# Layer 2 of a four-layer graph kernel: x2 turned on VectorE, h in x2's place, a seventh kept block, and another order of the last stores

## The chip, the cores and the metric

The kernel runs on one core of a Trainium2 chip. The metric is the device time of one execution in microseconds (us); lower is better. A core has TensorE (PE; its weight loads are listed as PEld), VectorE (DVE), ScalarE (ACT), GpSimd (POOL) and SyncE (SP), which here only issues transfers, on memory SBUF for operands and PSUM for matmul results. Transfers from every queue run on the core's 16 DMA engines.

## The reference

There are 3327 nodes of 64 features and one weighted adjacency `adj` of 3327 x 3327. Four layers follow each other, each ending in a residual and a layer norm. Cut to what matters:

```python
# layer 0:  x = LN(x + (1 - 0.1 * x - 0.01 * sum(x * (adj @ x))))
# layer 1:  hyperbolic attention over all pairs (i, j), weighted by
#           sigmoid(left_i + right_j) * adj
x = _layernorm(x + _L1_gnn_ref(x, adj, L1_gnn_att_W, L1_gnn_att_b))

# layer 2: two rounds over the whole adjacency
def _L2_gnn_ref(user_embs, adj, W):
    x = user_embs
    for k in range(2):
        agg = adj @ x
        x = jnp.tanh(jnp.concatenate([agg, x], axis=1) @ W[k])
    return x
x = _layernorm(x + _L2_gnn_ref(x, adj, L2_gnn_W))

# layer 3: the last 100 neighbours of each row, weights 0.5 ** (places from the end)
out = w @ (x @ weight) + bias
x = _layernorm(x + out)
```

## The kernel before

The host hands in the transposed adjacency, padded to 3328 x 3328: 26 blocks of 128 rows (the source nodes), each 128 partitions x 13312 bytes. A block is read from HBM several times: in layer 1, in both rounds of layer 2 and in layer 3. Some are kept in SBUF: `EARLY` = 4 blocks (25 to 22) from the beginning, and `LATE` = 2 blocks (20, 21) from the end of layer 1 until the end of layer 2.

Features are held in two forms: by node (128 nodes on the partitions, 26 x 64 values along a row) and stacked in columns (two halves of 64 features on the partitions, 1664 nodes along a row). `x2`, layer 1's result, is made by node in the last lines of `near_end` (L1554 to L1558) on VectorE; `lj` holds x2 times the first half of round 1's weights, made by TensorE and VectorE beside it.

**Layer 2** (`layers`, from L308) has two rounds, `k` = 0 and 1. Each adds up, in four PSUM chunks `acc[c]` of 416 nodes, one product per block and chunk (`add`, L400; two matmuls, one for each half of the nodes), so 26 blocks, and a part from the features themselves (`bottom`, L393: the second half of the weights times `hT`, x2 in columns). `tanh` (L493) writes h, the round's result, to `nxt`. `nxt` is a tile `hT` of the pool `cols` (two buffers of 128 x 1664 f32); layer 3's `accT` comes from the same pool.

In round 1 `hT` is x2 in columns and is written over the tile `xc` (`x2T`, L363): `turned(i)` (L383) transposes a group of three nodes' blocks on TensorE into PSUM, and ScalarE copies it out. Its five calls stand behind the fourth and fifth blocks, and `bottom` and a small Tanh (it loads the table) behind the sixth (L472 to L486).

Blocks that are not kept are streamed: four buffers in the pool `strm` (tag `at`, `UNDER_WAY` = 4), loaded ahead at the end of layer 1 by `blocks_ahead` (L1750), and two in the pool `more` (tag `bt`). The order of TensorE is written out by hand:

```python
order = list(ready)
for i, jb in enumerate(stay):
    order += [jb] + others[i * share : (i + 1) * share]
```

The `ready` blocks come first, then each kept block followed by `share` streamed ones; the blocks in `end` (two in round 1, three in round 2) are added chunk by chunk at the close, each chunk followed by its `tanh`. Before, round 1 is 0 to 3, 25, 4 to 7, 24, 8 to 11, 23, 12 to 15, 22, 16 to 19, and 20, 21 at the close: 16 streamed beside the four ready. Round 2 begins with the last six streamed blocks, which are still there, then 5 others, 20, 3 others, 21, 3 others, 25, 3 others, and closes with 24, 23, 22: 14 streamed. All loads stand in SP's queue in this order; a load waits until TensorE has consumed the block that lay in its buffer.

**Layer 1** (`near_sphere`, L989) runs over pairs of blocks and column chunks. Its left sides `lb` (128 x 3328 f32) are read by the sigmoid (L1052, listed as L1051) of each pair; the streamed half blocks `at` of the pool `n1r` (four buffers, on the right side of SBUF) are read by GpSimd (L1062). The order of its second half puts the kept blocks last, so no `at` is wanted in its last eight steps. The pools `late` and `strm` lie on the right, too, and take the room that layer 1's tiles leave.

**Layer 3's end** (`last_out`, L796) norms the last 1664 rows in three parts of 6, 4 and 3 node blocks and stores each; the last node block has only 127 rows and is stored alone (L828). `rsqrt_of` (L540) takes the root: one VectorE operation, ScalarE's Sqrt, a reciprocal and four VectorE operations.

Of the kernel before, what the change touches and what calls it, by code (L numbers as in the profile page):

```python
# [10 lines left out]
F32 = mybir.dt.float32  # L11
# [4 lines left out]
ALU = mybir.AluOpType  # L16
# [3 lines left out]
P = 128  # L20
# [17 lines left out]


EARLY = 4  # L40
LATE = 2
UNDER_WAY = 4

LN_EPS = 1e-5
MIN_NORM = 1e-15
# [28 lines left out]
def kernel(  # L74
# [232 lines left out]

    @with_exitstack  # L308
    def layers(ctx, x2, x3, begun_here, kept, ready, ahead_ctx, strm):
        cols = ctx.enter_context(tc.tile_pool(name="cols", bufs=2, reuse_waits="tile"))  # L310

        more_ctx = ExitStack()
        more = more_ctx.enter_context(tc.tile_pool(name="more", bufs=2, reuse_waits="tile"))
        l3m = None
        in_order = ctx.enter_context(ExitStack())
        in_order.enter_context(tc.manual_schedule(engines={mybir.EngineType.PE}))
# [20 lines left out]
            nc.vector.tensor_scalar(mask[q], at, 0.0, None, ALU.not_equal)  # L337

        groups = fours

        def to_stack(ps, src, dst, g, n, copy, name):

# [34 lines left out]
        with tc.tile_pool(name="l2p", bufs=2, space=PSUM, reuse_waits="tile") as l2p:  # L377
            for k in range(2):
                hw = lj
                nxt = cols.tile([P, HALF], F32, tag="hT", name=f"hT_{k + 1}")  # L380
                begun = set()

                def turned(i):  # L383
# [44 lines left out]
                if k == 0 and not begun_here:  # L428
                    turned(0)
                    turned(1)  # L430
                    top(0, nc.scalar.copy)
                    turned(2)
                    top(1)
                    for c in range(CPH):
                        add(c, order[0])
                    turned(3)
                    top(2)
                    turned(4)
                    top(3)
                    for c in range(CPH):  # L440
                        add(c, order[1])
                    top(4)
                    for c in range(CPH):
                        bottom(c)

                    warm_t = small.tile([P, 1], F32, tag="warm", name="warm_t")
                    nc.scalar.activation(warm_t, ones, AF.Tanh)
                    order = order[2:]
                elif k:
                    top(0)  # L450
                    bottom(0)
                    bottom(1)
                    top(1)
                    bottom(2)
                    for c in range(CPH - 1):
                        add(c, order[0])
                    top(2)
                    bottom(CPH - 1)
                    add(CPH - 1, order[0])
                    top(3)  # L460
                    order = order[1:]
                seen, held = {}, {}
                for i, jb in enumerate(order):
                    if jb not in blocks:
                        if len(seen) % (UNDER_WAY + 2) < 2 and (k == 0 or len(seen) < 2):
                            blocks[jb] = held[jb] = block(more, jb, tag="bt", name=f"bt_l2_{k}_{jb}")
                        else:
                            blocks[jb] = block(strm, jb, tag="at", name=f"at_l2_{k}_{jb}")
                        seen[jb] = blocks[jb]
                    for c in range(CPH):  # L470
                        add(c, jb)
                    if k == 0 and begun_here:  # L472

                        if i == 3:
                            turned(0)
                            turned(1)
                        if i == 4:
                            turned(2)
                            turned(3)
                            turned(4)  # L480
                        if i == 5:
                            for c in range(CPH):
                                bottom(c)

                            warm_t = small.tile([P, 1], F32, tag="warm", name="warm_t")
                            nc.scalar.activation(warm_t, ones, AF.Tanh)  # L486
                    if k and jb in held and len(held) == 2:
                        for q in range(AHEAD + 3):
                            masks(q)
                def chunk_end(c):  # L490
# [6 lines left out]
                for c in range(CPH):  # L497
                    chunk_end(c)

                last = sorted(list(seen)[-UNDER_WAY - 2 :], key=lambda jb: jb not in held)  # L500
                ready = {jb: seen[jb] for jb in last}
                hT = nxt

# [227 lines left out]

        def sums_out(h):

            accT = cols.tile([P, HALF], F32, tag="hT", name=f"accT_{h}")
            to = [
                accT[:, 2 * c * CW : 2 * (c + 1) * CW].rearrange("p (e k) -> p e k", e=2)
                for c in range(2)
            ]
            nc.scalar.activation(to[0], acc[h, 0], AF.Identity, bias=b3_sb)
            nc.vector.tensor_scalar(to[1], acc[h, 1], b3_sb, None, ALU.add)  # L740
            return accT
# [54 lines left out]
        def last_out(h, accT):  # L796

            xh, hh, sh = in_half(h)
            v = small.tile([P, NBH], F32, tag="v_out", name=f"v_out_{h}")
            parts = (slice(0, 6), slice(6, 10), slice(10, NBH))  # L800
            prs = [places(t) for t in (*banks, acc_tile(f"pr_o_{h}"))]
            for pr, s in zip(prs, parts):
                by_node(accT, pr, s)

            def added(k):
                s = parts[k]
                nc.vector.tensor_tensor(hh[:, s], prs[k][:, : s.stop - s.start], xh[:, s], ALU.add)
                nc.scalar.activation(sh[:, s], hh[:, s], AF.Square)

            def summed(k):  # L810
                s = parts[k]
                nc.vector.tensor_reduce(v[:, s], sh[:, s], axis=AX.X, op=ALU.add)

            added(0)
            added(1)
            summed(0)
            added(2)
            summed(1)
            summed(2)
            r = rsqrt_of(v, NBH)  # L820

            rows = N - h * HALF - (NBH - 1) * P
            for s, queue in zip(parts, (nc.sync, nc.scalar, nc.sync)):
                nc.vector.tensor_tensor(
                    hh[:, s], hh[:, s], spread(r[:, s], s.stop - s.start), ALU.mult
                )
                if store(queue, h, hh, s):
                    nc.scalar.dma_start(out[N - rows :], hh[:rows, NBH - 1])  # L828

        first_out = None  # L830
        with_step = [
# [42 lines left out]
    with tc.tile_pool(name="l1", bufs=1) as l1:  # L874
# [114 lines left out]
        def near_sphere(mT, ljT_0, xm, sq_e, t_e, rows_63):  # L989
# [3 lines left out]
            with tc.tile_pool(name="n1", bufs=1, reuse_waits="tile") as n1, tc.tile_pool(  # L993
# [1 line left out]
            ) as n1w, tc.tile_pool(  # L995
                name="n1c", bufs=1, space=PSUM, reuse_waits="tile"
            ) as n1c, ExitStack() as pairs:

                n1r = pairs.enter_context(
                    tc.tile_pool(name="n1r", bufs=4, side="right", reuse_waits="tile")  # L1000
                )
                first_ps = ExitStack()
                n1p = first_ps.enter_context(
                    tc.tile_pool(name="n1p", bufs=1, space=PSUM, reuse_waits="tile")
# [5 lines left out]
                ri = mT.rearrange("p (n d) -> p n d", d=D)  # L1010
                riT = n1.tile([P, HALF], F32, name="riT")

                lb = n1.tile([P, NP], F32, name="lb")
                lfT = n1.tile([NB, P], F32, name="lfT")
                lf_rows = dram.tile([NB, P], F32, name="lf_rows")

# [733 lines left out]
        def blocks_ahead(arm):  # L1750
# [6 lines left out]
                tc.tile_pool(name="strm", bufs=UNDER_WAY, side="right", reuse_waits="tile")  # L1757
            )
            all_kept, ready = dict(kept), {}
            for jb in range(NB - EARLY - LATE, NB - EARLY):  # L1760
                all_kept[jb] = block(late, jb, name=f"kept_{jb}")
            for jb in range(UNDER_WAY):
                ready[jb] = block(strm, jb, tag="at", name=f"at_l2_0_{jb}")
            return all_kept, ready, ahead_ctx, strm
# [60 lines left out]
```

## Time and profile before

| What | us |
|---|---|
| median of 3 runs | 561.71 |
| the runs | 560.8, 561.71, 563.36 |
| the profiled execution | 562.28 |
| its span, first to last instruction | 560.5 |
| TensorE busy | 527.3 (94%) |
| VectorE busy | 368.2 (66%) |
| ScalarE busy | 278.1 (50%) |
| GpSimd busy | 215.7 (38%) |
| layer 2's first block begins on TensorE | 241.93 |
| layer 2's second round, first block begins | 324.71 |
| layer 3's first product after layer 2 | 398.28 |

The mean granted TensorE clock was 0.987 of full speed. In the profile "L12" is line 12 of the kernel; a group is written as line, engine, operation, output <- inputs, shapes, and how often. An idle time is put down to the work that ended it ("<-"). Transfers moved 145.27 MB, 259 GB/s on average over the span. Times of single instructions count from the span's start.

### The profile page before, as it was taken

To read this page: it belongs to the slowest core of one execution; us is meant where nothing else is said; L and a number is where in the kernel's file an instruction comes from. 1 tells how busy PE (TensorE), PEld (TensorE's weight loads), DVE (VectorE), ACT (ScalarE), POOL (GpSimd) and SP (SyncE) were. 2 spreads that over 40 slices of the span, in tenths; PEclk is the share of its full clock that TensorE was granted. 3 is DMA by queue.
4 is the path that set the end of the run, shared out by engine and by line. 5 is a ranking of instruction groups with operands and counts; after the bars stand their busy time and mean duration, and the time that the engine had idled before them with its cause. 6 is when DMAs were issued, how large, how long until landed. Compare 5 with 4: busy or idle time off the path is not lost.

```text
span 560.5 us, 7513 instructions
## 1 busy us (share of the span) xinstructions
PE 527.3 (94%) x2854; PEld 226.6 (40%) x2854; DVE 368.2 (66%) x532; ACT 278.1 (50%) x328; POOL 215.7 (38%) x138
## 2 busy tenths in 40 slices
PE   8989989999999999999999999998989999999992
PEld 5522222222222222854444444443455555545542
DVE  6899999999999999791000011300478878787834
ACT  4899999999999998612000100000274333343311
POOL 3799999999999999200000000000011000000000
PEclk9899999999999999899999999999999999999997
DMA  8976766676766715699999149996609996789701
GB/s 305 353 273 205 234 209 204 222 233 199 238 205 223 235 32 222 272 425 425 425 426 424 43 148 417 425 425 291 244 8 343 342 303 227 237 258 358 274 2 36
DMA packets 34037, 145.27 MB, mean 259 GB/s; under 512 B 10285, under 2 KB 11975, under 8 KB 28871
## 3 DMA queue, kind: packets, MB, share of 16 engines
q1 hardware_dynamic: 31655, 144.11, 69.8%
q10 hardware_dynamic: 2336, 0.59, 0.5%
q8 instruction: 24, 0.39, 0.3%
q14 instruction: 22, 0.18, 0.1%
HBM read 143.23 MB, written 0.87 MB: 257 GB/s over the span
## 4 chain that ended last, share of the span: by engine, by line
PE 61%; DVE 20%; ACT 8%; DMA 6%; issue 3%; DVEq 0%
PE cnt L403 20%; PE pq L1075 12%; DVE v L1096 12%; PE cnt L513 11%; PE acc L709 6%; DMA at_l<-in_adjT 5%; ACT sg L1051 4%; PE acc L724 3%; ACT pq L1088 3%; DVE a L1087 2%; DVE w L526 1%; PE cnt L394 1%; DVE mask L337 1%; DMA x<-in_x 1%; PE pm L1367 1%
## 5 line engine op out<-in xcount | busy, mean ns | idle before, releaser
L1062 POOL TENSOR_TENSOR u<-sg,at 128x832 f32<-128x832 f32 x88 | 170.0, 1964 | 3.5 <-ACT sg L1051 3.0
L1075 PE MATMUL pq<-riT,ljT 64*128 64x416 f32 x416 | 100.2, 560 | 15.2 <-DVE v L1096 6.2
L1087 DVE SCALAR_TENSOR_TENSOR a<-pq,dl,u 128x832 f32<-128x832 f32 x104 | 111.9, 1077 | 2.9 <-PE pq L1075 2.8
L1088 ACT ACTIVATE pq<-pq,al,gas 128x832 f32<-128x832 f32 x104 | 105.0, 1011 | 15.1 <-DVE a L1087 14.2
L1096 DVE SCALAR_TENSOR_TENSOR v<-pq,a 128x832 f32<-128x832 f32 x104 | 105.7, 1016 | 1.1 <-ACT pq L1088 0.8
L1108 PE MATMUL acc<-v,xv 128*64 128x416 f32 x416 | 95.4, 537 | 0.1
L403 PE MATMUL cnt<-at_l,lj 128*64 128x416 f32 x480 | 86.1, 513 | 2.3 <-DMA at_l<-in_adjT 2.3
L1051 ACT ACTIVATE sg<-lb,rb 128x1664 f32<-128x1664 f32 (+1 forms) x53 | 87.3, 1647 | 0.1
L528 ACT ACTIVATE w<-cnt 128x832 int16<-128x832 f32 x55 | 47.3, 863 | 71.5 <-PE cnt L513 71.4
L640 POOL TENSOR_TENSOR s<-sq,s 128x384 bf16<-128x384 f32 (+1 forms) x4 | 4.1, 1028 | 200.3 <-ACT s L639 200.3
L493 ACT ACTIVATE hT<-cnt 128x416 f32<-128x416 f32 x8 | 4.1, 517 | 138.3 <-PE cnt L403 138.3
L1075 PEld LDWEIGHTS pq<-riT,ljT 64*128 64x128 f32 x416 | 31.5, 184 | 88.3 <-DVE v L1096 83.1
L526 DVE TENSOR_SCALAR w<-cnt 128x832 int16<-128x832 f32 x49 | 50.1, 1023 | 25.8 <-PE cnt L513 24.5
L403 PEld LDWEIGHTS cnt<-at_l,lj 128*64 128x64 f32 x480 | 34.1, 137 | 52.1 <-issue 47.3
L513 PE MATMUL cnt<-mask,tri 128*128 128x416 bf16 x208 | 53.5, 339 | 0.1
L709 PE MATMUL acc<-w,s 128*128 128x416 bf16 x208 | 52.6, 339 | 0.5 <-DVE hid L781 0.5
L513 PE MATMUL cnt<-mask,rest 128*128 128x416 bf16 x200 | 51.6, 340 | 1.2 <-ACT w L528 0.6
L391 DVE COPY lj<-pn_l 128x512 f32<-128x512 f32 (+1 forms) x4 | 2.4, 592 | 73.9 <-PE pn_l L355 73.9
L1108 PEld LDWEIGHTS acc<-v,xv 128*64 128x64 f32 x416 | 20.6, 134 | 61.0 <-issue 57.8
L337 DVE TENSOR_SCALAR mask<-ah 128x1664 bf16<-128x1664 f32 x42 | 43.4, 1034 | 0.0
L403 PE MATMUL cnt<-kept,lj 128*64 128x416 f32 x192 | 35.5, 514 | 0.0
L1062 POOL TENSOR_TENSOR u<-sg,kept 128x832 f32<-128x832 f32 x16 | 31.0, 1972 | 2.6 <-ACT sg L1051 2.6
(282 smaller groups left out, 403.7 us busy)
## 6 DMA issues: line engine op xcount, KB each, us to landing
at_l<-in_adjT SPq DMA_DIRECT2D x26, 1664.0 KB, 13.7
at<-in_adjT SPq DMA_DIRECT2D x44, 832.0 KB, 4.9
ah<-in_adjT SPq DMA_DIRECT2D x42, 832.0 KB, 6.3
bt_l<-in_adjT SPq DMA_DIRECT2D x8, 1664.0 KB, 12.8
kept<-in_adjT SPq DMA_DIRECT2D x6, 1664.0 KB, 8.7
lb<-lf_rows SPq DMA_DIRECT2D x2, 384.0 KB, 4.5
ljT<-ljT SPq DMA_DIRECT2D x4, 128.0 KB, 6.2
x<-in_x ACTq DMA_DIRECT2D x1, 416.0 KB, 5.5
```

The source lines that it names most:

```text
L337: nc.vector.tensor_scalar(mask[q], at, 0.0, None, ALU.not_equal)
L403: nc.tensor.matmul(acc[c][h * D : (h + 1) * D, :], hw[:, slot(jb), :], blocks[jb][:, o : o + CW], start=c not in begun, stop=last, skip_gr ...
L513: nc.tensor.matmul(cnt[c][:, e, :], mat, mask[q][:, of], start=start, stop=(mat is tri), skip_group_check=True,)
L526: nc.vector.tensor_scalar(w.bitcast(I16), cnt[c], 0.0, None, ALU.max)
L709: nc.tensor.matmul(acc[h, c][:, e, :], s12[:, slot(jb)].rearrange("p t d -> p (t d)"), ws[q, c][:, e, :], start=first, stop=last,)
L1051: nc.scalar.activation(sg[:, :, of], lbs[:, :, of], AF.Sigmoid, bias=rb[:, sl : sl + 1])
L1062: nc.gpsimd.tensor_tensor(u, sg[:, :, of], at[:, :, of], ALU.mult)
L1075: nc.tensor.matmul(pq[:, h, :], ljT[h != jb // NBH][rows, of], riT[rows, ch * CW : (ch + 1) * CW], start=True, stop=True,)
L1087: stt(a_s[t], pqs[t], dl[:, one], us.pop(t), op0=ALU.add, op1=ALU.mult)
L1088: nc.scalar.activation(pqs[t], pqs[t], AF.Square, bias=al[:, one], scale=gas[:, one])
L1096: stt(w, pqs.pop(t), CUBIC_REST, a_s.pop(t), op0=ALU.add, op1=ALU.mult)
L1108: nc.tensor.matmul(accs[cp, ci][h * D : (h + 1) * D, :], xv[:, slot(jb), :], w[:, h, :], start=(jb == orders[cp][0]), stop=(jb == orders[c ...
```

## The change

Six edits in one:

1. x2 is turned to columns by VectorE (`turned_by_squares`): sixteen instructions, each turning thirteen squares of 32 x 32 (32 partitions, 416 values). They stand at the head of round 1, behind x2's last addition on VectorE's queue. The TensorE transposes and ScalarE copies go. `bottom` moves behind the ninth block, and the small Tanh there reads a column of `hT`.
2. `cols` is no pool any more but another view of `x2`: both rounds' h and layer 3's `accT` are written there.
3. `LATE` is 3: block 19 is kept as well. Its place is that of `lb`, which moves to a pool of its own on the right beside `n1r`. The loads of 20 and 21 are issued first, then that of 19.
4. With that, `blocks_ahead` and `order` make other sequences. Round 1: 0 to 3, 25, 4 to 6, 24, 7 to 9, 23, 10 to 12, 22, 13 to 15, 20, 16 to 18, closing with 21, 19 (15 streamed). Round 2: six ready, 5 others, 20, 3 others, 21, 3 others, 19, 2 others, 25, closing with 24, 23, 22 (13 streamed).
5. In `last_out` the root is written out with one VectorE operation less, the factor -0.5 going into the last product.
6. The last three parts are multiplied and stored in the reverse order, and the 127 rows are stored first, on ScalarE's queue.

`MORE` = 2 only names a number that stood there.

```diff
--- before.py
+++ after.py
@@ -38,8 +38,9 @@
 
 
 EARLY = 4
-LATE = 2
+LATE = 3
 UNDER_WAY = 4
+MORE = 2
 
 LN_EPS = 1e-5
 MIN_NORM = 1e-15
@@ -307,10 +308,11 @@
 
     @with_exitstack
     def layers(ctx, x2, x3, begun_here, kept, ready, ahead_ctx, strm):
-        cols = ctx.enter_context(tc.tile_pool(name="cols", bufs=2, reuse_waits="tile"))
+
+        cols = x2.rearrange("p n d -> p (n d)")
 
         more_ctx = ExitStack()
-        more = more_ctx.enter_context(tc.tile_pool(name="more", bufs=2, reuse_waits="tile"))
+        more = more_ctx.enter_context(tc.tile_pool(name="more", bufs=MORE, reuse_waits="tile"))
         l3m = None
         in_order = ctx.enter_context(ExitStack())
         in_order.enter_context(tc.manual_schedule(engines={mybir.EngineType.PE}))
@@ -338,6 +340,20 @@
 
         groups = fours
 
+        def turned_by_squares(src, dst):
+
+            Q = 32
+            to = dst.rearrange("p (n k) -> p n k", k=P)
+            for h in range(2):
+                for f in range(D // Q):
+                    rows = slice(h * D + f * Q, h * D + (f + 1) * Q)
+                    for q in range(P // Q):
+                        nodes = slice(q * Q, (q + 1) * Q)
+                        nc.vector.transpose(
+                            out=to[rows, :, nodes],
+                            in_=by_half(src)[nodes, :, h, f * Q : (f + 1) * Q],
+                        )
+
         def to_stack(ps, src, dst, g, n, copy, name):
 
             pt = ps.tile([P, 4 * P], F32, tag="pt", name=f"pt_{name}_{g}")
@@ -377,7 +393,7 @@
         with tc.tile_pool(name="l2p", bufs=2, space=PSUM, reuse_waits="tile") as l2p:
             for k in range(2):
                 hw = lj
-                nxt = cols.tile([P, HALF], F32, tag="hT", name=f"hT_{k + 1}")
+                nxt = cols
                 begun = set()
 
                 def turned(i):
@@ -446,6 +462,8 @@
                     warm_t = small.tile([P, 1], F32, tag="warm", name="warm_t")
                     nc.scalar.activation(warm_t, ones, AF.Tanh)
                     order = order[2:]
+                elif k == 0:
+                    turned_by_squares(x2, hT)
                 elif k:
                     top(0)
                     bottom(0)
@@ -462,7 +480,7 @@
                 seen, held = {}, {}
                 for i, jb in enumerate(order):
                     if jb not in blocks:
-                        if len(seen) % (UNDER_WAY + 2) < 2 and (k == 0 or len(seen) < 2):
+                        if len(seen) % (UNDER_WAY + MORE) < MORE and (k == 0 or len(seen) < MORE):
                             blocks[jb] = held[jb] = block(more, jb, tag="bt", name=f"bt_l2_{k}_{jb}")
                         else:
                             blocks[jb] = block(strm, jb, tag="at", name=f"at_l2_{k}_{jb}")
@@ -471,20 +489,13 @@
                         add(c, jb)
                     if k == 0 and begun_here:
 
-                        if i == 3:
-                            turned(0)
-                            turned(1)
-                        if i == 4:
-                            turned(2)
-                            turned(3)
-                            turned(4)
-                        if i == 5:
+                        if i == 8:
                             for c in range(CPH):
                                 bottom(c)
 
                             warm_t = small.tile([P, 1], F32, tag="warm", name="warm_t")
-                            nc.scalar.activation(warm_t, ones, AF.Tanh)
-                    if k and jb in held and len(held) == 2:
+                            nc.scalar.activation(warm_t, hT[:, :1], AF.Tanh)
+                    if k and jb in held and len(held) == MORE:
                         for q in range(AHEAD + 3):
                             masks(q)
                 def chunk_end(c):
@@ -497,7 +508,7 @@
                 for c in range(CPH):
                     chunk_end(c)
 
-                last = sorted(list(seen)[-UNDER_WAY - 2 :], key=lambda jb: jb not in held)
+                last = sorted(list(seen)[-UNDER_WAY - MORE :], key=lambda jb: jb not in held)
                 ready = {jb: seen[jb] for jb in last}
                 hT = nxt
 
@@ -731,7 +742,7 @@
 
         def sums_out(h):
 
-            accT = cols.tile([P, HALF], F32, tag="hT", name=f"accT_{h}")
+            accT = cols
             to = [
                 accT[:, 2 * c * CW : 2 * (c + 1) * CW].rearrange("p (e k) -> p e k", e=2)
                 for c in range(2)
@@ -817,15 +828,25 @@
             added(2)
             summed(1)
             summed(2)
-            r = rsqrt_of(v, NBH)
+
+            r0, r = (small.tile([P, NBH], F32, tag=f"last_{k}", name=f"last_{k}") for k in range(2))
+            nc.vector.tensor_scalar(v, v, 1.0 / D, LN_EPS, ALU.mult, ALU.add)
+            nc.scalar.activation(r0, v, AF.Sqrt)
+            nc.vector.reciprocal(r0, r0)
+            nc.vector.tensor_tensor(r, v, r0, ALU.mult)
+            nc.vector.tensor_tensor(r, r, r0, ALU.mult)
+            nc.vector.scalar_tensor_tensor(r, r, -3.0, r0, op0=ALU.add, op1=ALU.mult)
 
             rows = N - h * HALF - (NBH - 1) * P
-            for s, queue in zip(parts, (nc.sync, nc.scalar, nc.sync)):
-                nc.vector.tensor_tensor(
-                    hh[:, s], hh[:, s], spread(r[:, s], s.stop - s.start), ALU.mult
+
+            for s, queue in zip(parts[::-1], (nc.sync, nc.scalar, nc.sync)):
+                nc.vector.scalar_tensor_tensor(
+                    hh[:, s], hh[:, s], -0.5, spread(r[:, s], s.stop - s.start),
+                    op0=ALU.mult, op1=ALU.mult,
                 )
-                if store(queue, h, hh, s):
+                if s.stop == NBH:
                     nc.scalar.dma_start(out[N - rows :], hh[:rows, NBH - 1])
+                store(queue, h, hh, s)
 
         first_out = None
         with_step = [
@@ -995,10 +1016,6 @@
             ) as n1w, tc.tile_pool(
                 name="n1c", bufs=1, space=PSUM, reuse_waits="tile"
             ) as n1c, ExitStack() as pairs:
-
-                n1r = pairs.enter_context(
-                    tc.tile_pool(name="n1r", bufs=4, side="right", reuse_waits="tile")
-                )
                 first_ps = ExitStack()
                 n1p = first_ps.enter_context(
                     tc.tile_pool(name="n1p", bufs=1, space=PSUM, reuse_waits="tile")
@@ -1010,7 +1027,14 @@
                 ri = mT.rearrange("p (n d) -> p n d", d=D)
                 riT = n1.tile([P, HALF], F32, name="riT")
 
-                lb = n1.tile([P, NP], F32, name="lb")
+                n1r = pairs.enter_context(
+                    tc.tile_pool(name="n1r", bufs=4, side="right", reuse_waits="tile")
+                )
+
+                n1l = pairs.enter_context(
+                    tc.tile_pool(name="n1l", bufs=1, side="right", reuse_waits="tile")
+                )
+                lb = n1l.tile([P, NP], F32, name="lb")
                 lfT = n1.tile([NB, P], F32, name="lfT")
                 lf_rows = dram.tile([NB, P], F32, name="lf_rows")
 
@@ -1757,8 +1781,12 @@
                 tc.tile_pool(name="strm", bufs=UNDER_WAY, side="right", reuse_waits="tile")
             )
             all_kept, ready = dict(kept), {}
-            for jb in range(NB - EARLY - LATE, NB - EARLY):
-                all_kept[jb] = block(late, jb, name=f"kept_{jb}")
+
+            first = NB - EARLY - LATE
+            at = {jb: late.tile([P, NP], F32, name=f"kept_{jb}") for jb in range(first, first + LATE)}
+            for jb in (*range(first + 1, first + LATE), first):
+                nc.sync.dma_start(at[jb], adjT[jb * P : (jb + 1) * P, :])
+                all_kept[jb] = at[jb]
             for jb in range(UNDER_WAY):
                 ready[jb] = block(strm, jb, tag="at", name=f"at_l2_0_{jb}")
             return all_kept, ready, ahead_ctx, strm
```

## The prediction

> **What bounds the kernel now.** I read the page first (shares and groups), then the chain that ended last in order of time, then the timeline of TensorE around the edit, then windows of the DMA share, and last the landing time of every block. Page, parts 4 and 5:
>
> ```profile
> PE 61%; DVE 20%; ACT 8%; DMA 6%; issue 3%; DVEq 0%
> ...
> L403 PE MATMUL cnt<-at_l,lj 128*64 128x416 f32 x480 | 86.1, 513 | 2.3 <-DMA at_l<-in_adjT 2.3
> ```
>
> TensorE carries the chain, and the 6% of DMA are layer 2's. The chain in order of time there (start, length, what):
>
> ```profile
> 295.23 16.83 DMA at_l<-in_adjT
> ...
> 312.10 8.60 PE cnt L403 x48
> ...
> 330.08 47.66 PE cnt L403 x272
> ...
> 377.76 13.34 DMA at_l<-in_adjT
> ...
> 391.15 7.20 PE cnt L403 x40
> ```
>
> Each of the two rounds ends on a transfer: its last block lands at 312.06 and at 391.10, and TensorE waits. How much: a block costs TensorE 2.79 us (block starts 286.64 and 300.60 have five blocks between them), so round 1's last streamed block could have begun at 311.77 and began at 312.10 (0.33 us); round 2's could have begun at 388.8 and began at 391.15 (2.3 us).
>
> The timeline of TensorE and its partners at the transposes (start, us, engine, line, operation):
>
> ```profile
> 253.18 0.87 PE L345 MATMUL pt_x<-ident,x 128*128 128x128 f32 x6
> ...
> 253.88 0.29 DVE L1558 TENSOR_TENSOR x<-x,xc 128x128 f32<-128x128 f32 x1
> ...
> 253.99 3.01 PE L403 MATMUL cnt<-kept,lj 128*64 128x416 f32 x16
> ...
> 256.93 0.87 PE L345 MATMUL pt_x<-ident,x 128*128 128x128 f32 x6
> ...
> 258.05 0.33 PE L345 MATMUL pt_x<-ident,x 128*128 128x128 f32 x1 [0.24 <-ACT xc L349]
> ...
> 258.31 3.01 PE L403 MATMUL cnt<-bt_l,lj 128*64 128x416 f32 x16
> ```
>
> Round 1 starts at 241.93; four blocks take it to 253.09, but the fifth begins at 253.99 (+0.90), and the sixth at 258.30 where 256.78 was due (+1.52). So the thirteen transposes of x2 cost TensorE 2.42 us. VectorE finishes x2 at 254.17 and is then free.
>
> Windows: in each, busy us of PE, PEld, DVE, ACT, POOL, the clock, the DMA share and GB/s:
>
> ```profile
> 207.00:219.50 12.50, 11.82 (x54) 3.18 (x52) 12.50 (x15) 11.49 (x11) 12.49 (x8) 1.00 0.70 274
> 219.50:227.50 8.00, 7.66 (x41) 3.08 (x41) 7.15 (x10) 5.17 (x7) 7.58 (x11) 1.00 0.00 0
> 229.00:308.00 79.00, 78.76 (x469) 40.14 (x469) 22.48 (x91) 10.84 (x28) 0.00 (x0) 0.98 1.00 421
> ```
>
> From 229 to 308 the DMA engines are full, and 219.5 to 227.5 they carry nothing. The landings say the same: round 1's stream lands at 236.10 and then every 4.00 us, the twentieth block at 312.06; round 2's at 336.60, 341.58, then every 4.00 us to 385.57, and the fourteenth at 391.10, 1.5 us late. Round 1 is a tie of TensorE and the stream: a change that only frees TensorE would gain 0.33 us there, one that only drops a transfer likewise. This one does both.
>
> [...]
>
> **The change part by part.**
>
> *Turns.* Removed: 13 transposes (2.42 us of TensorE) and five ScalarE copies (idle there anyway). Added: 16 VectorE turns of 32 partitions x 416 f32. Price: the addition of 128x416 f32 at L573 took 0.59 us; [...] 16 x 0.59 = 9.4, so from 254.2 to 263.6. Their reader, `bottom`, moves behind the ninth block, 241.93 + 9 x 2.79 = 267.1: covered by 3.5 us. Bounds: [...] twice the elements' share (L1552's 512 elements take 0.69 us, L1558's 384 take 0.56, so 416 are 0.42 of the 0.59): about 1.0 us, ending at 270.2, a stall of 3.1 us. I take 0.59. Behind the turns on VectorE's queue stands nothing until 321.8 (L391); behind the Tanh table load that now waits for them on ScalarE nothing until 316.6. `bottom` itself costs its 3.15 us (261.09 to 264.24) in either place.
>
> *Seventh kept block.* Block 19 is loaded before the stream, so 15 are streamed in round 1 beside the 4 ready, and 13 in round 2. It goes where `lb` lay; its last reader is L1051, ending at 219.34, so on SP's queue it follows the loads of 20 and 21 and moves between about 219.4 and 225.5, where the DMA is empty. On SP it stands ahead of the four stream loads, which wait for layer 1's end at 227.6 anyway. If this cover is gone, the whole stream is 4.0 us late. The nineteenth streamed block then lands at 308.1. TensorE without transposes wants it at 241.93 + 23 x 2.79 + 3.15 = 309.3. In the new order the tightest others are the seventh (lands 260.10, wanted 261.5) and the sixteenth (296.1, wanted 298.1): no wait. Slots come free in time (stream load 18 needs one freed at 289.8 and moves from 304). Round 1 gains 2.42 + 0.33 = 2.75 us.
>
> *Round 2.* It starts 2.75 us earlier, and its stream with it, since the first load waits for a block that TensorE consumes (329.71 before). Landings: thirteenth at 385.57 - 2.75 = 382.8, or 384.3 if the late 1.5 us of a last block come again. TensorE wants it as its 22nd block: 330.08 - 2.75 + 20 x 2.79 = 383.1. So the wait of 2.3 falls to between 0 and 1.2: gain 1.1 to 2.3, I take 1.7. Kept block 25 then follows, so the layer 3 loads that wait for the stream's buffers have 2.8 us more.
>
> *x2's place for h, accT.* No operation is added; all former readers are long done. The places of stream and l3 pools shift together. 0; if the shared buffer made a wait, it would be of ScalarE on a product ended 60 us before.
>
> *Last stores.* Windows of the tail, columns as above:
>
> ```profile
> 554.90:556.70 1.80, 0.00 (x0) 0.00 (x0) 0.00 (x0) 0.00 (x0) 0.00 (x0) 0.50 0.86 215
> 556.70:558.40 1.70, 0.00 (x0) 0.00 (x0) 0.00 (x0) 0.00 (x0) 0.00 (x0) 0.50 0.11 24
> ```
>
> The two stores on ScalarE's queue, from the timeline:
>
> ```profile
> 554.23 0.39 ACTq L764 DMA_DIRECT2D out<-hid  x1
> 554.71 0.59 ACTq L828 DMA_DIRECT2D out<-hid  x1
> ```
>
> Most data leaves by 556.7[...]. One small VectorE operation goes (pitch 0.20), and the short store is issued after the first product: 553.1 + 0.35 = 553.5 in place of 554.71. [...] Gain 0.5; bounds 0 (192 KB now leaves last) and 1.0.
>
> **Sum.** 2.75 + 1.7 + 0.5 = 4.95 us. The profiled execution took 562.28 (span 560.5 and 1.8 around it): 557.3. The median of the runs shown is 561.71, 0.57 below it: 556.8. Layer 3 between (412 to 546) repeats every 7.6 us on TensorE, so it only shifts.
>
> **Rivals.**
> A: *round 2's wait stays.* The last block straggles by more, or the earlier waits return; for it speaks the odd 1.5 us, against it 13 transfers where 14 were. Gain 2.75 + 0.5 = 3.25: 558.5.
> B: *the seventh block is late.* If the place of `lb` is free only with layer 1's other tiles at 227.6, the stream lands from 240.1 and ends at 312.1 with TensorE waiting; round 1 gains nothing, the rest 2.2: 559.5. Against it: the last reader at 219.34.
> C, the other sign: *the turns are dear.* Stall = 16t - 12.9. Above t = 0.81 us it begins, above 1.12 it eats all gains, above 1.29 the kernel is slower by over 0.5%. At 1.0: 559.9; at 1.5 us (11.1 of stall): 561.71 - 4.95 + 11.1 = 567.9. For it: no trace of such an operation, 4-byte data, 416 elements in runs of 32; [...]
>
> **How the numbers follow.** A measurement of this kernel can tell about 0.5%, 2.8 us. Forecast 0.62 (556.8, its own range 555.3 to 558.3), A 0.13 (558.5, mostly still beyond 0.5%, which is 558.9), B 0.08 (559.5, same), C 0.12: half of it at a stall of up to 3.1 (559.9, same), half slower; anything else 0.05. Faster 0.62 + 0.11 + a little = 0.75, same 0.18, slower 0.07. The range reaches from 555.2 (both bounds of gain, 2.75 + 2.3 + 1.0, and 0.5 of spread) to 560.2 (C at 1.0 us, 559.9, and a little spread).
>
> **What would show it.** No `pt_x` products after 242; sixteen VectorE turns of 0.5 to 0.6 us ending near 264; `bottom` at about 267 with no wait on VectorE; kept_19 landing by 226 and the stream's first still at 236; round 1's last streamed block starting near 309.4 without a DMA wait; round 2's DMA wait at or below 1.2 us; the short store's rows gone from the end, and the tail from the last product to the span's end 0.3 to 0.6 shorter. Turns of 1 us or more, a stream that lands 4 us later, or a wait of over 2 us in round 2 would make it wrong.

## The result, and the profile after

The changed kernel takes 559.64 us (median of 7 runs, 558.98 to 560.16) beside 561.82 us before: a ratio of 0.9957 with a 95% interval of 0.9939 to 0.9975, so 2.2 us between the medians, under half of the 4.95 us forecast. The time lies in the forecast range of 555.2 to 560.2 by luck: the upper end was meant for turns that cost 1.0 us each, and these cost 0.63. The profiled execution took 559.12 us, its span 557.4.

The page of the changed kernel, parts 4 and 5:

```profile
PE 66%; DVE 20%; ACT 8%; issue 3%; DMA 1%; DVEq 0%
...
L419 PE MATMUL cnt<-at_l,lj 128*64 128x416 f32 x448 | 80.2, 513 | 0.0
```

DMA has fallen from 6% of the chain to 1%, and the products on the streamed `at_l` blocks (448 where 480 were) have no idle time ahead of them. The chain of the changed kernel in order of time (start, length, what):

```profile
243.08 25.29 PE cnt L419 x144
268.37 2.99 PE cnt L410 x8
271.36 47.64 PE cnt L419 x272
...
328.38 65.79 PE cnt L419 x376
```

Both pieces of DMA are gone: TensorE carries both rounds without a break. Nine blocks, `bottom`, seventeen blocks: round 1 needs nothing else. The timeline of the turns and their reader in the changed kernel (start, us, engine, line, operation):

```profile
255.03 0.29 DVE L1582 TENSOR_TENSOR x<-x,xc 128x128 f32<-128x128 f32 x1
...
255.36 10.11 DVE L352 STREAM_TRANSPOSE xc<-x 32x416 f32<-32x416 f32 x16
...
263.59 0.20 ACT L497 ACTIVATE warm_t<-xc 128x1 f32<-128x1 f32 x1 [20.60 <-DVE xc L352]
...
268.30 3.06 PE L410 MATMUL cnt<-xc,w_dg 128*128 128x416 f32 x8
```

Sixteen turns took 10.11 us, 0.63 us each, and ended at 265.47; `bottom` began at 268.30 with no wait on VectorE, so 2.8 us of cover were left. Windows of the changed kernel (us, busy of PE, PEld, DVE, ACT, POOL, the clock, the DMA share, GB/s):

```profile
220.40:228.40 8.00, 7.65 (x42) 3.00 (x40) 7.41 (x10) 5.31 (x8) 7.66 (x11) 1.00 0.57 213
229.00:308.00 79.00, 79.00 (x472) 40.57 (x472) 33.27 (x108) 9.57 (x25) 0.00 (x0) 0.98 0.98 411
```

The seventh block moves (DMA share 0.57) where before's DMA engines stood empty (0.00 from 219.5 to 227.5), and TensorE is busy for all 79 us of the second window.

The program is one chain of stages that only shift, so the span can be cut at five places: first `v` of layer 1, first product of layer 2, last tanh of round 1, first product of layer 3, ScalarE's last copy into `accT` (its start). Us, worked out from the traces' instructions:

```
                         before    after    difference
start of layer 1          23.17    24.39      +1.22
layer 1                  218.69   218.62      -0.07
round 1 of layer 2        78.89    76.04      -2.85
round 2 of layer 2        77.53    75.06      -2.47
layer 3                  148.00   147.99      -0.01
tail, to the span's end   14.17    15.28      +1.11
sum                      560.45   557.38      -3.07
```

Layer 2 gained 5.3 us, more than forecast. Two places that no step of the forecast had as a loss gave 2.3 us back: the start and the tail.

In the tail the data left as forecast. The last stores on ScalarE's queue in the changed kernel, with the short store first:

```profile
549.30 0.50 ACTq L848 DMA_DIRECT2D out<-hid  x1
549.90 0.59 ACTq L775 DMA_DIRECT2D out<-hid  x1
```

The last landing came 12.69 us after the last `accT` (554.79 less 542.10) where before it came 13.20 after it (559.48 less 546.28): 0.5 us earlier. But the span went on. Two views of the semaphore waits with which SyncE closes the changed program; each line has the number of instructions, their shortest, median and longest duration in ns, and the first and last start:

```profile
L1849 SPq EVENT_SEMAPHORE  x2: 28/28/28, 554.1 to 554.2; - x2
...
L1849 SPq EVENT_SEMAPHORE  x6: 28/28/28, 556.1 to 556.5; - x6
```

SyncE runs two of its eight closing waits and then does nothing for 1.9 us (554.20 to 556.14), though everything that it waits for has landed by 554.79. In the kernel before the first six run in one go:

```profile
L1821 SPq EVENT_SEMAPHORE  x6: 28/28/28, 558.3 to 558.7; - x6
...
L1821 SPq EVENT_SEMAPHORE  x2: 28/28/28, 559.5 to 559.6; - x2
```

There the gap ahead of the last two is the wait for the last landing at 559.48. In the changed kernel it is not: the window from 554.80 to the end shows no engine at work and a DMA share of 0.01:

```profile
554.80:557.38 2.58, 0.00 (x0) 0.00 (x0) 0.00 (x0) 0.00 (x0) 0.00 (x0) 0.50 0.01 3
```

The compiled programs differ in length there. The program has two arms behind an `If` on a flag read at run time, of which only the first runs here; `any_norm`, used below, belongs to the other. SyncE's program has 866 instructions before and 864 after, since the seventh block saves a load in each arm. In both kernels SyncE also stands still between its last branch and its first closing wait, for 3.3 us before (555.04 to 558.33) and 3.5 after (550.55 to 554.09). That the length of SyncE's program also makes the gap among the closing waits was at this point the author's guess, called the theory of the code's place in the expectations; the experiments test it.

### The profile page after: what moved, and what is told of

It is laid out like the page before. It is cut to its first block, busy times and chain, and to the rows that moved or that the text cites. A ratio compares the mean times of both kernels' runs of the same rounds, so it can differ in the third digit from the quotient of the medians.

```text
span 557.4 us, 7490 instructions
## 1 busy us (share of the span) xinstructions
PE 525.1 (94%) x2841; PEld 226.5 (41%) x2841; DVE 377.8 (68%) x547; ACT 276.2 (50%) x323; POOL 215.5 (39%) x138
## 4 chain that ended last, share of the span: by engine, by line
PE 66%; DVE 20%; ACT 8%; issue 3%; DMA 1%; DVEq 0%
PE cnt L419 25%; PE pq L1099 12%; DVE v L1120 12%; PE cnt L524 11%; PE acc L720 6%; ACT sg L1075 4%; PE acc L735 3%; ACT pq L1112 3%; DVE a L1111 2%; DVE w L537 1%; PE cnt L410 1%; DVE mask L339 1%; DMA x<-in_x 1%; PE x_w L1435 1%; PE pn_l L371 1%
## 5 line engine op out<-in xcount | busy, mean ns | idle before, releaser
L419 PE MATMUL cnt<-at_l,lj 128*64 128x416 f32 x448 | 80.2, 513 | 0.0
L504 ACT ACTIVATE x<-cnt 128x416 f32<-128x416 f32 x8 | 4.1, 517 | 130.6 <-PE cnt L419 130.6
L419 PEld LDWEIGHTS cnt<-at_l,lj 128*64 128x64 f32 x448 | 31.9, 137 | 46.0 <-issue 45.2
L419 PE MATMUL cnt<-kept,lj 128*64 128x416 f32 x224 | 41.2, 513 | 0.0
```

The source lines that it names most:

```text
L419: nc.tensor.matmul(acc[c][h * D : (h + 1) * D, :], hw[:, slot(jb), :], blocks[jb][:, o : o + CW], start=c not in begun, stop=last, skip_gr ...
```

## The experiments

Each is an edit of one of the two kernels. Stages by the same cuts as above (us; "start" is the first `v` of layer 1), medians of runs with before's on the same chip, and the ratio with its interval, which is taken over the runs and differs from the quotient of the medians by up to 0.0006:

```
                start  round 1  round 2   tail   median  before  ratio [95%]
e1_turns        23.46   78.77    79.60   14.27   561.87  561.85  0.9996 [0.9983, 1.0009]
e2_seventh      23.08   78.52    75.42   15.53   561.31  561.85  0.9996 [0.9985, 1.0008]
e3_tail         24.50   78.72    77.52   13.66   561.43  561.85  0.9992 [0.9981, 1.0004]
e4_shift        23.47   76.04    75.06   13.72   556.99  561.85  0.9918 [0.9901, 0.9935]
e5_old_tail     23.15   76.04    75.09   15.52   558.81  561.89  0.9959 [0.9946, 0.9972]
e6_seventh_sh.  23.16   78.52    75.24   13.86   560.41  561.89  0.9977 [0.9964, 0.9990]
e7_placebo      23.02   78.73    77.42   15.37   563.21  561.89  1.0030 [1.0016, 1.0044]
e8_early_bott.  23.15   84.29    75.08   13.64   564.86  561.89  1.0063 [1.0050, 1.0076]
r1_after        23.02   76.04    75.06   15.47   558.57  561.73  0.9951 [0.9934, 0.9967]
r2_shift        23.15   76.04    75.37   13.67   557.45  561.73  0.9932 [0.9915, 0.9949]
r3_seventh      23.21   78.52    75.14   14.39   560.78  561.73  0.9982 [0.9974, 0.9991]
b1_before       23.34   78.62    76.81   13.82   560.98 (one run)
b2_before       23.15   78.77    77.31   13.85   561.39 (one run)
b3_before       23.41   78.66    77.47   14.27   562.20 (one run)
b4_after        23.18   76.04    75.92   15.47   558.93 (one run)
```

**The turns alone** (before, with VectorE's turns and `bottom` behind the ninth block; blocks and stores as before):

```
+                elif k == 0:
+                    turned_by_squares(x2, hT)
...
-                        if i == 5:
+                        if i == 8:
                             for c in range(CPH):
                                 bottom(c)
```

> Only the turns go to VectorE (with bottom behind the ninth block); six kept blocks, two buffers for h, the old last stores. Theory (a tie of TensorE and the stream): TensorE is free 2.4 us earlier in round 1, but the twentieth streamed block still lands where it did, so the last streamed block begins where it did, and round 1 from its first block to its last tanh keeps 78.9 us, round 2 its 77.5: 0.0 us against before, within 0.5. Rival (TensorE alone bounds round 1): round 1 is 2.4 us shorter and the kernel with it. Theory of the code's place: SP's program has as many instructions as before, so no second stall at its end and a tail of 14.2 us from the last accT to the span's end.

Measured 0.9996: nothing. (Round 2 of its profile, 79.60, holds 3.40 us at a granted clock of 0.50; see the last section.) The chain of this kernel shows why (start, length, what):

```profile
293.05 19.19 DMA at_l<-in_adjT
...
312.28 8.60 PE cnt L417 x48
```

The twentieth streamed block still lands at 312.24, and what TensorE saves becomes a wait for the last blocks (2.1 us in all in round 1). Half of the forecast's remark on the tie was wrong: freeing TensorE alone gains 0, not 0.33 us. The work taken away there lies ahead of a transfer that is as late as ever.

**The seventh block alone** (before, with `LATE = 3`, h in x2's place and `lb` where block 19 can take its room; TensorE's transposes and the old stores):

```
-LATE = 2
+LATE = 3
...
-        cols = ctx.enter_context(tc.tile_pool(name="cols", bufs=2, reuse_waits="tile"))
+        cols = x2.rearrange("p n d -> p (n d)")
```

> Only the seventh kept block, with x2's place for h and accT and lb on the right; TensorE still turns x2, the last stores are as before. Theory: round 1 loses only its wait of 0.33 us, so 78.5; round 2 loses its whole wait, so about 75.1 (before 77.5): 2.8 us less in layer 2. Theory of the code's place: SP's program is two instructions shorter than before, as in the changed kernel, so the waits at its end stall a second time, after the second of them, and the tail is about 0.8 us longer than before's 14.2 (the last landing hides the rest). Sum about -2.0 us. Rival for the tail (the reverse order of the stores made it longer): tail 14.2, sum -2.8. Rival for layer 1 (lb on the right makes its head 1.2 us longer): 1.2 us more than either[...].

Its rounds are 78.52 and 75.42 (78.5 and 75.1 expected), but the time did not move clear of the noise (0.9996; 0.5 us between the medians where 2.0 was expected). SyncE's program has 864 instructions here too, and the tail is 15.53, longer by 1.3 us where 0.8 was expected. **The last stores alone** keep 866:

```
-            for s, queue in zip(parts, (nc.sync, nc.scalar, nc.sync)):
+            for s, queue in zip(parts[::-1], (nc.sync, nc.scalar, nc.sync)):
```

> Only the last part: the root with one operation less, and the reverse order of the stores. Theory of the code's place: SP's program is as long as before, so there is one stall behind the branch and none within the waits; the last landing comes 0.5 us earlier, the tail from the last accT to the end is 13.4 to 13.8 us (before 14.2), and the kernel 0.4 to 0.8 us faster. Rival (storing 192 KB last makes the end later): tail about 15.3 us as in the changed kernel, 1.1 us slower.

The tail is 13.66. Before's tail in four profiles is 14.17, 13.82, 13.85 and 14.27 (the first and b1 to b3), 14.03 in the mean, so the new last stores are worth about 0.4 us there; in the whole time that does not stand clear of the noise (0.9992). They are not what lengthened the tail. **The changed kernel with eight more loads of one value in the arm that is not taken** (the padded kernel) executes nothing more; SyncE's program grows from 864 to 879 instructions:

```
         def any_norm(m, x1):
+            for _ in range(8):
+                nc.sync.dma_start(attb_sb, att_b.partition_broadcast(P))
```

> The changed kernel with eight small loads on SP's queue added in the arm of the branch that is not run: nothing more is executed, but SP's program is 15 instructions longer[...]. Theory of the code's place: the second stall of 2.0 us is gone, the tail is 13.6 to 13.9 us in place of 15.3, and the kernel is 1.4 to 1.7 us faster than the changed one, so about 4 us faster than before. Rival (order of the stores): tail 15.3, no difference from the changed kernel (ratio to before 0.9957).

> The changed kernel with the eight loads in the arm that is not taken, once more, beside the run above. My theory: rounds of 76.0 and 75.1 us and a tail of 13.7 us again, 556.8 to 557.5 us. The rival, that its gain over the changed kernel was in part the luck of its runs: 557.8 us or more.

Both times the tail is 13.7 and the kernel takes 556.99 and 557.45 us, 0.9918 and 0.9932 of before. SyncE's closing waits of the first of these runs:

```profile
L1851 SPq EVENT_SEMAPHORE  x7: 28/28/28, 553.3 to 554.0; - x7
```

These seven run through without the gap, and the eighth follows at once. The counter-test is **the kernel before with 118 such loads**, which give 992 instructions and again execute nothing more. The length is 128 above the changed kernel's 864; that 128 more would bring the gap back was the author's guess:

```
         def any_norm(m, x1):
+            for _ in range(118):
+                nc.sync.dma_start(attb_sb, att_b.partition_broadcast(P))
```

> The kernel before with 118 loads of one value added on SyncE in the arm that is not taken: nothing more is executed, and SyncE's program grows from 866 to 992 instructions[...]. My theory: both rounds as in before (78.9 and 77.5 us), but a second stall between the closing waits, a tail of 15.3 to 15.6 us in place of 14.2, and the time 1.2 to 1.4 us above before. The rival, that what is not executed costs nothing: a tail of 14.2 us and the same time.

Slower by 1.3 us between the medians (1.0030, interval 1.0016 to 1.0044), rounds unchanged, tail 15.37. SyncE's closing waits of this kernel:

```profile
L1823 SPq EVENT_SEMAPHORE  x2: 27/28/28, 557.8 to 557.9; - x2
...
L1823 SPq EVENT_SEMAPHORE  x6: 28/28/28, 559.9 to 560.2; - x6
```

The gap of the changed kernel, at the same two waits, in the old kernel. So the tail goes with the length of SyncE's program, in both directions (13.72 us beside 15.28 in e4_shift, 15.37 beside 14.17 in e7_placebo), though what is added never runs. With 864 and 992 instructions the gap stands at the same two waits; with 866 and 879 it is not there. What SyncE does in the gap no view names. **The changed kernel with the old stores** (864 instructions) agrees:

```
-            for s, queue in zip(parts[::-1], (nc.sync, nc.scalar, nc.sync)):
+            for s, queue in zip(parts, (nc.sync, nc.scalar, nc.sync)):
```

> The changed kernel with the last stores of before (order, queues and the one small VectorE operation as they were); SyncE's program has 864 instructions, as in the changed kernel. My theory, that the tail's loss belongs to where SyncE's closing waits lie in its program and not to the stores: round 1 takes 76.0 us and round 2 75.1 us as in the changed kernel, the tail from the last copy to the span's end is 15.3 to 15.7 us [...], and the time is about 3.9 us below before, some 0.4 us above the changed kernel at a like head of the run. The rival, that the new order of the stores lengthens the tail: the tail is 14.2 us and the time about 5.3 us below before.

Its tail is 15.52 beside 15.28 to 15.47 of the changed kernel. With the second gap at the end the 0.4 us of the stores are mostly hidden behind it. The median, 3.1 us below before, came short of the 3.9 expected.

**The seventh block alone with the eight loads**, in two runs:

> The seventh block alone, without VectorE's turns and with the old tail, plus eight loads of one value on SyncE in the arm that is not taken, so that nothing more is executed [...]. My theory: round 1 78.5 us and round 2 75.4 us as in the kernel with the seventh block alone, tail 14.2 us in place of 15.5, and the time about 2.5 us below before (0.3 of round 1, 2.1 of round 2). The rival, that the seventh block is worth little by itself however the tail falls (it came out at 0.2 us in the median): no more than 1.5 us below before.

> The seventh block alone with the eight loads, once more. Its profile gained 3.1 us over before's, its median only 1.5 us, and its runs lay from 559.1 to 562.2 us. My theory: in some executions TensorE's clock is halved for 3.4 us behind a wait in a round, which the profiled execution escaped; the runs spread over 2 us or more again, with a median 1 to 2 us below before, and where the profile catches such a stretch, the round with it is 1.5 to 2.2 us longer. The rival, that the executions differ at the start only: rounds of 78.5 and 75.2 us again, and a spread of 1.3 us or less.

The tail falls to 13.86 and 14.39 from 15.53, and the kernel becomes faster (0.9977 and 0.9982), which it was not, clear of the noise, without the loads. So the gain was lost in the tail. The size is not settled: 1.5 and 0.95 us where 2.5 was expected. The runs of the second spread over 2.3 us, but the rounds of its profile (78.52 and 75.14) hold none that is longer by the 1.5 to 2.2 us of a halved stretch, so my reason for the spread is not shown.

**The price of the turns' cover** (the changed kernel with the eight loads, and `bottom` behind the sixth block):

```
-                        if i == 8:
+                        if i == 5:
```

> The changed kernel with the eight loads in the arm not taken, and with the two-row products that read the turned half issued behind the sixth block of round 1 in place of the ninth. My theory, that VectorE's turns are hidden only by the blocks ahead of their reader: the sixth block ends 16.7 us into round 1 and the turns 22.5 us into it, so TensorE waits about 5.7 us for VectorE there, round 1 takes 81.7 us in place of 76.0, round 2 stays at 75.1, and the time is about 1 us above before (4.6 below, plus 5.7). The rival, that the wait is made good because the stream of blocks runs ahead meanwhile and round 1 is bound by the stream too: round 1 at most 78 us.

The wait is there, 5.54 us, and none of it is made good. The cost is larger: round 1 takes 84.29 us, 8.25 more. The timeline and a window of it:

```profile
264.26 5.70 PE L410 MATMUL cnt<-xc,w_dg 128*128 128x416 f32 x8 [5.54 <-DVE xc L352]
```

```profile
262.80:269.60 6.80, 5.34 (x8) 2.53 (x8) 1.34 (x3) 0.00 (x0) 0.00 (x0) 0.50 1.02 431
```

The granted clock is 0.50 from 262.80, while TensorE still waits, to 269.60, and `bottom` takes 5.70 us in place of 3.06. The missing 2.7 us are that.

**What the medians hold.** The profiled executions of before and after differ by 3.1 us with an unlucky start, and by 4.3 without it; the medians by 2.2 and 3.2. Both kernels were run again:

> The changed kernel once more, as it is, beside the next run on the same chip. The two profiles so far differ in two things: the tail (15.28 against 13.72 us) and the start of layer 1 (24.39 against 23.47 us, where TensorE's clock was halved for 6.8 us in place of 3.4). My theory: the tail's 1.5 us are steady and the start is chance, so that profiles fall at 23.1 to 23.5 or at 24.4 to 24.5 whatever the kernel, and the medians of the two kernels differ by 1.5 to 2.0 us. The rival, that the change itself lengthens the start: 24.4 again, and medians apart by 2.5 us or more.

> The kernel before once more, for a second profile. Its profile so far and those of the kernels that share its rounds put the two rounds at 78.9 and 77.5 us, the tail at 14.2; yet its executions spread from 560.2 to 563.6 us, and between the profiled executions the change gains 4.3 us, between the medians 2.2 to 3.2. My theory: the spread comes from TensorE's halved stretches, at the start (one or two of them, 1.2 us) and behind the wait in round 2 (2.1 us where one falls there). The rival: the wait in round 2 itself differs, and in quick executions its last block is not late, round 2 taking 76.3 us or less.

> As the run ahead of it, for a third profile: the start at 23.1 to 23.5 or at 24.4 to 24.5 us, and round 2 at 77.4 to 77.6 or, with a halved stretch behind its wait, at 79.5 us; the rival has round 2 at 76.3 us or less.

> As the two runs ahead of it, for a fourth profile: my theory round 2 at 77.4 to 77.6 or 79.5 us, the rival 76.3 us or less.

> The changed kernel for a third profile: rounds of 76.0 and 75.1 us again, since no wait is left in them, a tail of 15.3 to 15.5 us, and the start at 23.1 to 23.5 or 24.4 to 24.5 us. The rival, that some executions of it too are longer in the rounds: round 1 or 2 above these by 0.5 us or more.

The start is chance: 23.02 and 23.18 in two more profiles of the changed kernel. Of 17 profiles of all kernels two have it at 24.4 to 24.5 (one of a kernel with before's layer 1) and fifteen at 23.0 to 23.5; in the changed kernel's first profile, one of the two late ones, the granted clock is 0.50 for 6.8 us (12.04 to 18.86), in before's first for 3.4 (13.85 to 17.26), in that of e4_shift for 3.4. The medians of the changed and the padded kernel lie 1.1 us apart on one chip, below the 1.5 to 2.0 expected.

Round 2 is not steady. For before the rival had that in kind, though not in size (76.81 where it said 76.3 or less); for after the rival of the last run came true (75.92, 0.86 above the first profile). The longest waits of TensorE in the first further run of before, and in the last of after (total, times, longest):

```profile
PE cnt L403 <- DMA at_l<-in_adjT: 1.3, 1, 1.3
```

```profile
PE cnt L419 <- DMA at_l<-in_adjT: 0.6, 1, 0.6
```

In four profiles of before the waits of round 2 come to 2.1, 1.3, 2.0 and 2.0 us; in three of after to 0, 0 and 0.6, there for a block before the last. The profile that the forecast was made from has the longest of four. What makes a block late by more in one execution than in another stays open.

With the means of all profiles of the two kernels (before four, after three), start and layer 1 left out since they carry only chance:

```
           before   after    difference   forecast
round 1     78.74   76.04      -2.70       -2.75
round 2     77.28   75.35      -1.93       -1.7
tail        14.03   15.41      +1.38       -0.5
sum                            -3.25       -4.95
```

The sum agrees with the 3.2 us between the medians of the second comparison. The 2.2 us of the first stay a us short of it; the start's 1.2 us, where they fall, would fill that, but how often they fell in those runs is not shown.

## Why the prediction was right or wrong

**Turns: right.** 0.63 us each where 0.59 was taken, the author's estimate from an addition of 128x416 f32, and 1.0 the upper bound; layer 2 began 1.15 us later in this profile, and so reckoned they ended at 264.3 (263.6 forecast) and `bottom` began at 267.15 (267.1). Rival C, the dear turn, needed 0.81. Where the step put a missing cover at "a stall of 3.1 us", it counted the wait alone; e8_early_bottom shows that a wait of 5.5 us cost 8.25. The Tanh table load did not wait for the turns: it took 1.28 us from 241.71, and only the Tanh behind it waited.

**Seventh block: right.** Reckoned the same way its load was issued at 219.4 and landed at 226.3, the stream began as before, the nineteenth streamed block landed at 307.95 (308.1 forecast), and round 1 gained 2.85 in the first profile and 2.70 in the mean beside 2.75. Rival B is refuted. Only the aside on the tie failed, in the half that e1_turns tried; the other half held, 78.52 beside 78.89 for the seventh block without the turns, 0.37 us (0.22 against the mean of four).

**Round 2: right in mechanism, and in the mean inside its bounds of 1.1 to 2.3.** Reckoned as above, the last streamed block landed at 382.6 (382.8 forecast) and TensorE did not wait for it. The gain is 1.93 in the mean, and 2.47, beyond the bound, between the first two profiles; that the mean lies so near to the 1.7 is in part luck, since the step took its wait from the longest of four. Rival A's straggling block appears in one of three profiles, with 0.6 us.

**x2's place for h and `accT`: right.** Layer 1 and layer 3 are unchanged to 0.1 us.

**Last stores: the step that failed.** The data left earlier, as it said: the last landing came 0.5 us earlier than in the first profile of before and 0.4 earlier than in the mean of four (12.69 us behind the last `accT` beside 13.06), and where SyncE's waits run through (e3_tail, e4_shift, r2_shift) the tail is 13.7, 0.3 to 0.4 below before. What failed is the step's last sentence, the gain of 0.5 us (the author's estimate) at the end of the span, since it took the last landing for the end and put what stands behind it at nothing. Behind it stand SyncE's closing waits, and the load that the seventh block saves in each arm shortened SyncE's program by two instructions, which opened a gap of 1.9 us between them. The term measured +1.38 in place of -0.5: 1.9 us. Of the forecast's 4.95 that leaves 3.1, and 3.25 is what the stages add up to; the one us from there to the 2.2 of the medians stays open.

The padded kernel shows the rest of the sum without that gap: its rounds and tail average 76.04, 75.22 and 13.70 in two profiles, which is 5.1 us below before's, and its medians are 4.9 and 4.3 below: 556.99 and 557.45 us beside the 556.8 forecast. It is 1.1 us below the changed kernel side by side (the two intervals overlap there).

**Chances.** No case among mine was "SyncE stands still among its closing waits", nor did the range reach up to 560.2 for it; the profile of before showed the 3.3 us in which SyncE stood still behind its last branch, and the step read the same stretch only as stores.

## What to carry to other kernels

Where a chain of work ties with a stream of transfers, shorten both or neither moves: the turns alone gave 0 and the block alone 0.2 to 0.4 us of round 1, together 2.7. In a kernel that stores until its end, look at what the engine that closes the program does behind the last store: two instructions fewer, or 126 more that never run, moved the end by 1.3 us here, as much as the smaller edits being tried. Take a difference of a us from several executions, stage by stage: the first profile of the changed kernel was off by 1.2 us at the start, and round 2 differed by 0.7 and 0.9 us between profiles of one kernel.

## What the runs showed of the hardware

Instructions that are never executed changed the time, by +1.3 us in the kernel before (e7_placebo) and by -1.1 and -2.65 between the medians of the changed and the padded kernel (1.3 and 2.5 between their profiled spans; the larger pair was not run side by side, and has the late start in it).

In e1_turns a stretch of halved clock stood behind a wait of 2.31 us for round 2's last block:

```profile
391.69 4.71 PE L417 MATMUL cnt<-at_l,lj 128*64 128x416 f32 x16 [2.31 <-DMA at_l<-in_adjT]
```

```profile
392.00:395.40 3.40, 3.40 (x12) 1.20 (x10) 0.00 (x0) 0.00 (x0) 0.00 (x0) 0.50 0.00 0
```

The block took 4.71 us in place of the 2.96 of another in the same kernel, and round 2 was 2.1 us longer than in the first profile of before, where a like wait of 2.1 us was followed by no such stretch (the granted clock there is 1.00 from 391.20 to 398.00). The wait in e1_turns and the 1.75 us that the block took longer come to 4.06 us, 1.8 times the wait. The changed kernel, which has no wait or one of 0.6 us in its rounds, showed no such stretch there: the clock is 1.00 from 243.1 to 394.2 in its first profile, r1_after repeats the rounds of that profile (76.04 and 75.06 us), and b4_after, with the wait of 0.6, has 76.04 in round 1 and a clock of 1.00 from 317 to 395. What decides whether a halved stretch stands behind a wait is not shown.
